# Edge attributes turned by VectorE in 32x32 squares, from rows loaded to two sets of partitions

## Chip, core and metric

The kernel runs on one core of one Trainium2 chip. The metric is the device time of one execution in microseconds; the lower the better. The median of three runs of the kernel before is 1333.0 us (1331.73 to 1334.65).

Names used below: PE or TensorE multiplies matrices, and its weight loads (PEld) run beside the matmuls; DVE or VectorE works on elements; ACT or ScalarE computes activations and copies; POOL or GpSimd here issues the gathers; SP or SyncE issues most of the other transfers. PSUM is the memory that TensorE writes[...].

## What is computed

A graph layer over 8192 nodes of 256 features and 131072 edges of 64 attributes. The edges are sorted by their target node.

```python
ea  = edge_attr @ w_e + b_e                       # 131072 x 256
msg = relu(x[src] + ea)                           # rows of x gathered by source node
agg = segment_sum(msg, dst, num_segments=8192)    # summed by target node
t = x + agg
h_local = bn1(relu(t @ w1 + b1) @ w2 + b2 + x)
# attention within graphs of 32 nodes, 4 heads
q, k, v = split(x.reshape(256, 32, 256) @ in_w.T + in_b)
h_attn = bn2((softmax(q k' / 8) v) @ out_w.T + out_b + x)
out = h_local + h_attn
out = bn3(out + relu(out @ m_w1 + m_b1) @ m_w2 + m_b2)
return layernorm(x + out)
```

All arrays are float32.

## The kernel before

**Two kinds of work.** The edges are cut into 128 blocks of 1024 (NB, BE), the nodes into 16 chunks of 512 (NCH, CH). A block is 4 groups (NH) of 256 edges; a group is 128 partitions by TJ = 2 edges. The node work of a chunk is attention (attention_front, attention_back) and, after all sums for its nodes have been placed, the dense layers (dense).

**An edge block, in five steps.** gather (L129) issues 8 indirect loads on POOL, each of 128 rows of x, into one of 4 buffers xs. load_edges (L144) issues on SP, for every second block, one load of 512 KB that brings the attributes of two blocks, 512 contiguous bytes (two edges) for each partition and group; there are two such buffers. edge_transpose (L163) turns the four 128x128 squares of a block by TensorE into one PSUM bank (tag "sm"), from where ScalarE copies them to eaT, of which there are two buffers. edge_products (L451) multiplies eaT, half of the partitions for each of the two edges, with w_e (matmuls at L459) into two-bank tiles "pe", of which there are two; for the first NX = 20 blocks it also adds b_e by matmuls at L467, and later blocks gather from xb, a copy of x with b_e added that copy_load and copy_store make in the first 14 blocks. edge_messages (L472) adds the gathered rows to the products on VectorE (L481, two additions of 128x1024 per block, four of 128x512 in the last) and applies relu on ScalarE (L485). edge_sums (L497) adds the messages of equal targets by matmuls with a 0/1 matrix oh (edge_hot, L490), into a bank of the same tag "sm"; ScalarE copies them to ws. edge_place (L516) spreads these sums over node columns by matmuls at L522 into a bank l2 of its own, and VectorE adds them to xT, the turned x of the chunk (L532).

**Order.** TensorE's order is written out by hand for the whole loop, that of VectorE and ScalarE up to block NV = 26; elsewhere a scheduler orders the instructions when the kernel is built. The loop goes in rounds of two blocks up to block 119 and of one block from 120 on (NS = 8). A round consists of products, messages, the sums of the blocks of the round before, products and messages of the second block, node work, transposes for two blocks ahead, placing of the sums, and node work.

**The planner.** Node work is cut into steps that are Python generators; each step yields its TensorE time in the planner's own microseconds (1.7 for a layer's 512 columns, for instance). `work.run(us)` takes steps from four streams in turn until the time asked for is used up. A step that yields REST lets its stream rest for two calls of run. Each round asks for 0.3 of its share, then twice 0.1 around the transposes and the placing, then 0.5 (PER = 5.1 for a block). A chunk's dense layers are ready when the last block that touches its nodes has been placed.

**PSUM.** Two banks "at" for node work, two tiles "pe" of two banks, one bank "sm" shared by edge_transpose and edge_sums, one bank l2.

**Start.** The source nodes of the first two blocks are loaded to the layout of the gathers by two small DMAs (L61). Those of all other blocks are loaded as rows, converted (srcf), turned by TensorE and copied to srci; the targets likewise (dstf to rel).

Of the kernel before, what the change touches and what calls it, by code (L numbers as in the profile page):

```python
# [18 lines left out]
P = 128  # L19
# [8 lines left out]
TB = NH * TJ  # L28
NPB = N // NB
# [22 lines left out]
def gnn_kernel(ctx: ExitStack, tc: tile.TileContext, x, src, dst, edge_attr, w, out):  # L52
# [7 lines left out]
    for b in range(ND):  # L60
        (nc.sync, nc.scalar)[b].dma_start(  # L61
            srcd[:, b * NH : (b + 1) * NH, :], src[b * BE : (b + 1) * BE].rearrange("(g p j) -> p g j", p=P, j=TJ)
        )
# [56 lines left out]
    def bank():  # L120
        return pps.tile([P, CH], FP, name="at", tag="at", bufs=2)
# [22 lines left out]
    def load_edges(b):  # L144

        if b % 2:
            return
        ea = epool.tile([P, 2, NH, TJ * ED], FP, name="ea", tag="ea", bufs=2)
        nc.sync.dma_start(
            ea.rearrange("p s h d -> p (s h) d"),  # L150
            edge_attr[b * BE : (b + 2) * BE, :].rearrange("(g p j) d -> p g (j d)", p=P, j=TJ),
        )
        for s in range(2):
            ea_of[b + s] = ea[:, s]
# [4 lines left out]
    load_edges(2)  # L159
# [3 lines left out]
    def edge_transpose(b):  # L163
        ea = ea_of.pop(b)
        tp = pps.tile([P, NH, P], FP, name="tp", tag="sm", bufs=1)
        for h in range(NH):
            nc.tensor.transpose(tp[:, h, :], ea[:, h, :], ident)  # L167
        eaT = epool.tile([P, NH, P], FP, name="eaT", tag="eaT", bufs=2)
        nc.scalar.copy(eaT, tp)  # L169
        eaT_of[b] = eaT  # L170

    with tc.tile_pool(name="setup", bufs=1) as sp:
# [17 lines left out]
        edge_transpose(0)  # L190
        edge_transpose(1)
        srcf = npool.tile([P, NH, P, TJ], FP, name="srcf", tag="zT")
        nc.vector.tensor_copy(srcf.rearrange("s h p j -> s (h p j)"), srci_r)
        for h in range(NH):
            ps = bank()[:, : TJ * NB].rearrange("p (j s) -> p j s", j=TJ)
            for j in range(TJ):
                nc.tensor.transpose(ps[:, j, :], srcf[:, h, :, j], ident)
# [33 lines left out]
        dstf = npool.tile([P, NH, P, TJ], FP, name="dstf", tag="oT")  # L231
        nc.vector.tensor_copy(dstf.rearrange("s h p j -> s (h p j)"), dsti_r)

        dst3 = dstf.rearrange("s h p j -> s h (p j)")
# [5 lines left out]
        for h in range(NH):  # L240
            ps = bank()[:, : TJ * NB].rearrange("p (j s) -> p j s", j=TJ)
            for j in range(TJ):
                nc.tensor.transpose(ps[:, j, :], dstf[:, h, :, j], ident)
# [207 lines left out]
    def edge_products(b):  # L451

        eaT = eaT_of.pop(b)
        for h in range(0, NH, 2):
            pe = bank2().rearrange("p i (u c) -> p i u c", u=2)
            for u in range(2):
                for i in range(2):
                    rows = slice(i * ED, (i + 1) * ED)
                    nc.tensor.matmul(  # L459
                        pe[:, i, u, :], eaT[rows, h + u, :], we[rows, :],  # L460
# [9 lines left out]
            pe_of[b, h] = pe  # L470

# [343 lines left out]
```

## Time and profile before

One execution was profiled: it took 1332.57 us, and its span from the first instruction to the last is 1330.7 us.

| engine | busy us | share of the span | instructions |
|---|---|---|---|
| PE | 1234.3 | 93% | 8307 |
| PEld | 783.6 | 59% | 8307 |
| DVE | 712.2 | 54% | 1202 |
| ACT | 658.7 | 49% | 959 |
| POOL | 983.9 | 74% | 1032 |

| row of the profile | count | busy us | mean us of one |
|---|---|---|---|
| L134 gather (from xb; from x 160 more) | 864 | 824.9 | 0.955 |
| L481 message addition, DVE | 258 | 304.7 | 1.211 |
| L459 edge product, PE | 2048 | 262.3 | 0.391 (overlapping) |
| L504 sums, PE | 2048 | 124.6 | 0.382 (overlapping) |
| L169 copy of turned attributes, ACT | 128 | 74.3 | 0.581 |

The DMA engines moved 206.8 MB, 155 GB/s over the span.

How to read this: busy time is time in which an instruction of the engine was running; matmuls overlap, so that the mean duration of one times their count is more than their busy time. A timeline line gives start, duration, engine, line, operation, what it writes and reads, and in brackets how long the engine was idle before it and which event ended that. "issue" means that the profile shows no event. Several instructions of one kind can stand in one line (x4); the duration is then that of all. An engine that is idle costs nothing where another sets the pace.

### The profile page before, as it was taken

The numbers are of one execution on the slowest core, as the hardware profiler recorded it, in microseconds if no ns is written. First come the engines' busy times: TensorE is split into PE (matmuls) and PEld (weight loads), VectorE is DVE, ScalarE is ACT, GpSimd is POOL, SyncE is SP. The second block draws the span as 40 slices with busy tenths as digits, with TensorE's granted clock in tenths as the row PEclk, the third lists the DMA queues.
The fourth block names the chain that finished last, engine by engine and source line by source line (L and its number), as shares of the span: only waits on it lengthen the run. The fifth ranks groups of instructions, "written<-read, shape, count | busy, mean of one in ns | idle before, by whom it ended". The sixth has DMA issues, their size and how long they took to land.

```text
span 1330.7 us, 21178 instructions
## 1 busy us (share of the span) xinstructions
PE 1234.3 (93%) x8307; PEld 783.6 (59%) x8307; DVE 712.2 (54%) x1202; ACT 658.7 (49%) x959; POOL 983.9 (74%) x1032
## 2 busy tenths in 40 slices
PE   4998979999999999899899999999898998989997
PEld 3766756655555556556556565555555565655665
DVE  4566554555537464644637464564636446454654
ACT  2535344465546455455546555463545445544443
POOL 7777777777777777777777777777777777777770
PEclk9998989999999999999999999999999999999999
DMA  8788655454545454454545454454445445444540
GB/s 279 251 277 272 198 149 151 135 159 130 168 137 153 135 166 126 132 170 125 165 137 150 138 169 136 121 169 138 151 138 151 135 138 150 136 136 139 159 116 30
DMA packets 140613, 206.77 MB, mean 155 GB/s; under 512 B 19646, under 2 KB 103900, under 8 KB 139740
## 3 DMA queue, kind: packets, MB, share of 16 engines
q0 software_dynamic: 49152, 134.28, 35.0%
q1 hardware_dynamic: 89468, 69.76, 16.8%
q10 hardware_dynamic: 1888, 1.32, 0.3%
q8 instruction: 67, 1.10, 0.3%
q14 instruction: 38, 0.31, 0.1%
HBM read 188.51 MB, written 16.78 MB: 154 GB/s over the span
## 4 chain that ended last, share of the span: by engine, by line
PE 56%; POOL 17%; issue 9%; DVE 8%; ACT 6%; DMA 4%; DVEq 0%; ACTq 0%; POOLq 0%
POOL xs L134 17%; PE at L391 16%; PE pe L459 11%; PE at L294 6%; PE pw L504 5%; PE l L522 3%; PE at L372 3%; DVE msg L481 3%; PE at L308 3%; PE tp L167 3%; PE pe L467 3%; DMA xs<-xb,srci 2%; PE at L360 2%; ACT pr L335 2%; DVE bd L352 1%
## 5 line engine op out<-in xcount | busy, mean ns | idle before, releaser
L134 POOL DMA_INDIRECT xs<-xb,srci x864 | 824.9, 955 | 263.8 <-issue 249.8
L485 ACT ACTIVATE msg<-msg 128x1024 f32<-128x1024 f32 (+1 forms) x258 | 270.9, 1051 | 329.5 <-DVE msg L481 320.7
L481 DVE TENSOR_TENSOR msg<-pe,xs 128x1024 f32<-128x1024 f32 (+1 forms) x258 | 304.7, 1211 | 174.5 <-PE pe L459 72.3
L459 PE MATMUL pe<-we,eaT 64*128 64x256 f32 x2048 | 262.3, 391 | 12.0 <-DVE msg L481 11.1
L459 PEld LDWEIGHTS pe<-we,eaT 64*128 64x128 f32 x2048 | 187.3, 187 | 99.7 <-issue 43.5
L134 POOL DMA_INDIRECT xs<-in_x_dram,srci x144 | 142.1, 987 | 45.3 <-issue 41.1
L391 PE MATMUL at<-hA,mw 128*128 128x512 f32 (+2 forms) x304 | 123.6, 533 | 3.4 <-ACT xT L284 2.0
L504 PE MATMUL pw<-msg,oh 128*32 128x256 f32 x2048 | 124.6, 382 | 0.0
L169 ACT COPY eaT<-tp 128x512 f32<-128x512 f32 x128 | 74.3, 581 | 100.0 <-PE tp L167 99.4
L294 PE MATMUL at<-xT,inT 128*128 128x512 f32 x256 | 122.7, 605 | 1.1 <-ACT xT L284 1.1
L391 PE MATMUL at<-m,mw 128*128 128x512 f32 (+2 forms) x304 | 117.4, 530 | 1.4 <-ACT m L407 1.4
L532 DVE TENSOR_TENSOR xT<-l,xT 128x352 f32<-128x352 f32 (+4 forms) x98 | 43.2, 463 | 96.0 <-PE l L522 96.0
L167 PEld LDWEIGHTS tp<-ident,ea 128*128 128x128 f32 x512 | 63.8, 144 | 49.9 <-issue 39.3
L504 PEld LDWEIGHTS pw<-msg,oh 128*32 128x32 f32 x2048 | 59.6, 109 | 54.6 <-issue 21.9
L167 PE MATMUL tp<-ident,ea 128*128 128x128 f32 x512 | 80.0, 280 | 11.8 <-DMA ea<-in_edge_attr_dram 6.1
L522 PEld LDWEIGHTS l<-oh,ws 128*128 128x128 f32 x512 | 74.1, 191 | 14.9 <-issue 13.5
L522 PE MATMUL l<-oh,ws 128*128 128x160 f32 x512 | 81.8, 301 | 0.5 <-ACT ws L510 0.5
L391 PEld LDWEIGHTS at<-m,mw 128*128 128x128 f32 x304 | 53.8, 190 | 48.0 <-issue 43.8
L391 PEld LDWEIGHTS at<-hA,mw 128*128 128x128 f32 x304 | 52.6, 190 | 49.1 <-issue 39.2
L294 PEld LDWEIGHTS at<-xT,inT 128*128 128x128 f32 x256 | 46.1, 192 | 50.2 <-issue 47.2
L391 PE MATMUL at<-xT,w 128*128 128x512 f32 (+2 forms) x152 | 64.8, 558 | 10.1 <-DVE y L431 4.7
L391 PE MATMUL at<-h,w 128*128 128x512 f32 (+2 forms) x152 | 65.5, 554 | 9.1 <-ACT h L398 6.4
(109 smaller groups left out, 1286.9 us busy)
## 6 DMA issues: line engine op xcount, KB each, us to landing
ea<-in_edge_attr_dram SPq DMA_DIRECT2D x64, 512.0 KB
xs<-xb,srci POOLq DMA_INDIRECT x864
xn<-in_x_dram SPq DMA_DIRECT2D x16, 512.0 KB
out_dram<-y SPq DMA_DIRECT2D x14, 512.0 KB
xp<-in_x_dram SPq DMA_DIRECT2D x10, 512.0 KB
xb<-xp SPq DMA_DIRECT2D x10, 512.0 KB
xp<-in_x_dram SPq DMA_DIRECT2D x3, 1024.0 KB
xb<-xp SPq DMA_DIRECT2D x3, 1024.0 KB
```

The source lines that it names most:

```text
L134: nc.gpsimd.indirect_dma_start(out=xs[:, h, j, :], out_offset=None, in_=x if b < NX else xb[:, :], in_offset=bass.IndirectOffsetOnAxis(ap= ...
L167: nc.tensor.transpose(tp[:, h, :], ea[:, h, :], ident)
L169: nc.scalar.copy(eaT, tp)
L294: nc.tensor.matmul(ps, inT[:, k, o * P : (o + 1) * P], xT[:, k, :], start=(k == 0), stop=(k == KC - 1))
L308: nc.tensor.matmul(ps[:, (t - t0) * C : (t - t0 + 1) * C], xT[:, k, t * P : (t + 1) * P], inT[:, k, 2 * C :], start=(k == 0), stop=(k == K ...
L391: nc.tensor.matmul(ps, wt[:, k, o * P : (o + 1) * P], act[:, k, :], start=(k == 0), stop=(k == nk - 1))
L459: nc.tensor.matmul(pe[:, i, u, :], eaT[rows, h + u, :], we[rows, :], start=(b >= NX or u == 0), stop=(b >= NX), skip_group_check=True,)
L481: nc.vector.tensor_add(msg[:, hs].rearrange("p u i c -> p i u c"), pe[:, :, u : u + n, :], xs[:, hs].rearrange("p u i c -> p i u c"),)
L485: nc.scalar.activation(msg[:, hs], msg[:, hs], AF.Relu)
L504: nc.tensor.matmul(pw[h * WN : (h + 1) * WN, i, :], oh[:, h * TJ + j, :], msg[:, h, j, :], start=(j == 0), stop=(j == TJ - 1), skip_group_ ...
L522: nc.tensor.matmul(l2[:, k, i * NPB : i * NPB + WB], ws[:, i, k * P : (k + 1) * P], oh2[:, i, :], start=(i == 0 and k == 0), stop=(i == la ...
L532: nc.vector.tensor_add(xT, l2[:, :, a - n : z - n], xT)
```

## The change

load_edges now loads one block at a time, in four DMAs of 32 partitions. Each DMA brings all four groups of the edges of one j, 1 KB (four edges) per partition and group. The same rows go to two sets of 32 partitions, once for the first 32 attributes (i = 0) and once for the last 32 (i = 1); the second set lies 32 columns further left, so that one access pattern finds the right half on all partitions. The loaded bytes are twice those of before. edge_transpose is now one VectorE instruction that turns all 32x32 squares of the block from ea to eaT; TensorE and ScalarE have no part in it. With the new layout, partition p of a group of 128 edges stands for edge r*4+m and no longer for pairs of edges, so the source and target indices are loaded and turned in the matching order.

The transposes are issued right behind the products that free their eaT buffer (next_edges), and the load for two blocks later behind them. The bank "sm" is gone: edge_sums and edge_place share the one bank of tag "pw", and "at" has three banks. The two calls `work.run(0.1 * per)` are one call `work.run(0.2 * per)`.

```diff
+QR = 32
+EQ = P // QR
...
     for b in range(ND):
-        (nc.sync, nc.scalar)[b].dma_start(
-            srcd[:, b * NH : (b + 1) * NH, :], src[b * BE : (b + 1) * BE].rearrange("(g p j) -> p g j", p=P, j=TJ)
-        )
+        for m in range(EQ):
+            (nc.sync, nc.scalar)[m % 2].dma_start(
+                srcd[m * QR : (m + 1) * QR, b * NH : (b + 1) * NH, :],
+                src[b * BE : (b + 1) * BE].rearrange("(g j r m) -> m r g j", j=TJ, r=QR, m=EQ)[m],
+            )
...
     def bank():
-        return pps.tile([P, CH], FP, name="at", tag="at", bufs=2)
+        return pps.tile([P, CH], FP, name="at", tag="at", bufs=3)
...
     def load_edges(b):
-        if b % 2:
-            return
-        ea = epool.tile([P, 2, NH, TJ * ED], FP, name="ea", tag="ea", bufs=2)
-        nc.sync.dma_start(
-            ea.rearrange("p s h d -> p (s h) d"),
-            edge_attr[b * BE : (b + 2) * BE, :].rearrange("(g p j) d -> p g (j d)", p=P, j=TJ),
-        )
-        for s in range(2):
-            ea_of[b + s] = ea[:, s]
+        ea = ea_of[b] = epool.tile([P, QR + NH * EQ * ED], FP, name="ea", tag="ea", bufs=2)
+        for j in range(TJ):
+            for i in range(ED // QR):
+                p0, c0 = j * ED + i * QR, (1 - i) * QR
+                nc.sync.dma_start(
+                    ea[p0 : p0 + QR, c0 : c0 + NH * EQ * ED].rearrange("r (g d) -> r g d", g=NH),
+                    edge_attr[b * BE : (b + 1) * BE, :].rearrange("(g j r m) d -> j r g (m d)", j=TJ, r=QR, m=EQ)[j],
+                )
...
     def edge_transpose(b):
         ea = ea_of.pop(b)
-        tp = pps.tile([P, NH, P], FP, name="tp", tag="sm", bufs=1)
-        for h in range(NH):
-            nc.tensor.transpose(tp[:, h, :], ea[:, h, :], ident)
-        eaT = epool.tile([P, NH, P], FP, name="eaT", tag="eaT", bufs=2)
-        nc.scalar.copy(eaT, tp)
-        eaT_of[b] = eaT
+        eaT = eaT_of[b] = epool.tile([P, NH * EQ, QR], FP, name="eaT", tag="eaT", bufs=2)
+        nc.vector.transpose(eaT, ea[:, QR:].rearrange("p (g d) -> p g d", d=ED)[:, :, :QR])
...
-        edge_transpose(0)
-        edge_transpose(1)
-        srcf = npool.tile([P, NH, P, TJ], FP, name="srcf", tag="zT")
-        nc.vector.tensor_copy(srcf.rearrange("s h p j -> s (h p j)"), srci_r)
+        for b in range(2):
+            edge_transpose(b)
+            load_edges(b + 2)
+        srcf = npool.tile([P, NH * TJ, EQ, QR], FP, name="srcf", tag="zT")
+        nc.vector.tensor_copy(srcf, srci_r.rearrange("s (t r m) -> s t m r", r=QR, m=EQ))
...
+    def next_edges(b):
+        if b < NB:
+            edge_transpose(b)
+        if b + 2 < NB:
+            load_edges(b + 2)
...
-        pw = pps.tile([P, 2, C], FP, name="pw", tag="sm", bufs=1)
+        pw = pps.tile([P, 2, C], FP, name="pw", tag="pw", bufs=1)
...
-        l2 = pps.tile([P, KC, C], FP, name="l2", tag="l2", bufs=1)
+        l2 = pps.tile([P, KC, C], FP, name="l2", tag="pw", bufs=1)
...
             for i in blocks:
-                if i % 2 == 0 and i + 4 < NB:
-                    load_edges(i + 4)
                 if i + 2 < NB:
                     gather(i + 2)
...
             edge_products(b)
+            next_edges(b + 2)
             edge_messages(b)
             if waiting:
                 sums = edge_sums(waiting)
             waiting = list(blocks)
             if n == 2:
                 edge_products(b + 1)
+                next_edges(b + 3)
                 edge_messages(b + 1)
...
-            for k, i in enumerate(blocks):
-                if i + 2 < NB:
-                    edge_transpose(i + 2)
-                    if k == 0:
-                        work.run(0.1 * per)
-                if sums and k == 0:
-                    edge_place(*sums)
-                    placed, sums = sums[0][-1], None
-                    work.run(0.1 * per)
+            if sums:
+                edge_place(*sums)
+                placed, sums = sums[0][-1], None
+            work.run(0.2 * per)
             for i in blocks:
                 edge_hot(i)
             work.run(0.5 * per)
```

The targets (dstf) are converted and turned like the sources; edge_products reads the same 128 columns per group from the new eaT.

More of the change, by code (lines that the diff above doesn't have):

```diff
@@ L158, in gnn_kernel @@
     gather(1)
-    load_edges(2)
+    load_edges(1)
     eaT_of = {}
@@ L196, in gnn_kernel @@
             for j in range(TJ):
-                nc.tensor.transpose(ps[:, j, :], srcf[:, h, :, j], ident)
+                nc.tensor.transpose(ps[:, j, :], srcf[:, h * TJ + j].rearrange("s m r -> s (m r)"), ident)
             nc.vector.tensor_copy(srci[:, :, h * TJ : (h + 1) * TJ].rearrange("p s j -> p j s"), ps)
@@ L228, in gnn_kernel @@
         turned(out_r, outT, KC)
-        dstf = npool.tile([P, NH, P, TJ], FP, name="dstf", tag="oT")
-        nc.vector.tensor_copy(dstf.rearrange("s h p j -> s (h p j)"), dsti_r)
-        dst3 = dstf.rearrange("s h p j -> s h (p j)")
+        dstf = npool.tile([P, NH * TJ, EQ, QR], FP, name="dstf", tag="oT")
+        nc.vector.tensor_copy(dstf, dsti_r.rearrange("s (t r m) -> s t m r", r=QR, m=EQ))
+        dst3 = dstf.rearrange("s (h j) m r -> s h (j m r)", j=TJ)
         lo = sp.tile([P, NH], FP, name="lo")
@@ L242, in gnn_kernel @@
             for j in range(TJ):
-                nc.tensor.transpose(ps[:, j, :], dstf[:, h, :, j], ident)
+                nc.tensor.transpose(ps[:, j, :], dstf[:, h * TJ + j].rearrange("s m r -> s (m r)"), ident)
             nc.vector.tensor_copy(rel[:, :, h * TJ : (h + 1) * TJ].rearrange("p s j -> p j s"), ps)
@@ L451, in edge_products @@
     def edge_products(b):
-        eaT = eaT_of.pop(b)
+        eaT = eaT_of.pop(b).rearrange("p (h m) r -> p h (m r)", h=NH)
         for h in range(0, NH, 2):
@@ L459, in edge_products @@
                     nc.tensor.matmul(
-                        pe[:, i, u, :], eaT[rows, h + u, :], we[rows, :],
+                        pe[:, i, u, :], eaT[rows, h + u], we[rows, :],
                         start=(b >= NX or u == 0), stop=(b >= NX), skip_group_check=True,
```

## Prediction

> **What bounds the kernel now.** I read the page's first part, then who waited for whom on GpSimd (POOL), then POOL's timeline from its first gather to its last, then VectorE beside it, and last the timeline of the end.
>
> ```profile
> PE 1234.3 (93%) x8307; PEld 783.6 (59%) x8307; DVE 712.2 (54%) x1202; ACT 658.7 (49%) x959; POOL 983.9 (74%) x1032
> ...
> L134 POOL DMA_INDIRECT xs<-xb,srci x864 | 824.9, 955 | 263.8 <-issue 249.8
> ```
>
> TensorE looks like the bound (93%), POOL has 74%. But POOL's busy time leaves out 0.3 us in front of every gather, and those gaps end with no releaser ("issue"). The waits of POOL say the same:
>
> ```profile
> POOL xs L134 <- issue: 295.5, 970, 0.3
> POOL xs L134 <- DVE oh L513: 3.8, 6, 1.7
> ```
>
> 970 of 1024 gathers start 0.3 us behind the one before; all other waits of POOL together are some 17 us, and most of these too are the same 0.3 us under another name. Only one is long: 1.7 us, in front of block 18. In POOL's timeline (start, duration) the first gathers and the last are
>
> ```profile
> 3.31 1.10 POOL L134 DMA_INDIRECT xs<-in_x_dram,srcd  x1 [1.70 <-DMA srcd<-in_src_dram]
> 4.71 0.95 POOL L134 DMA_INDIRECT xs<-in_x_dram,srcd  x1 [0.31 <-issue]
> ```
> ```profile
> 1298.82 0.94 POOL L134 DMA_INDIRECT xs<-xb,srci  x1 [0.30 <-issue]
> ```
>
> One gather each 1.25 us. From 3.31 to 1299.76 are 1296.5 us; 1024 x 1.25 = 1280; the other 16.5 are gathers that took longer and two waits for a free xs buffer. So the time is 3.3 (start) + 1296.5 (gathers) + 30.9 (end) = 1330.7 us, and what the change takes from TensorE counts only where it shortens one of the three. Which gathers take longer? Those that start inside a VectorE operation with two SBUF inputs; four stream transposes in a row hold none:
>
> ```profile
> 61.87 3.42 DVE L552 TENSOR_TENSOR xp<-xp,be 128x2048 f32<-128x2048 f32 x2
> 62.71 2.26 POOL L134 DMA_INDIRECT xs<-in_x_dram,srci  x1 [0.30 <-issue]
> ```
> ```profile
> 173.16 2.85 DVE L352 STREAM_TRANSPOSE bd<-pr 32x512 f32<-32x512 f32 x4
> ```
> ```profile
> 173.07 0.94 POOL L134 DMA_INDIRECT xs<-in_x_dram,srci  x1 [0.30 <-issue]
> 174.31 0.94 POOL L134 DMA_INDIRECT xs<-in_x_dram,srci  x1 [0.30 <-issue]
> ```
>
> The gather at 62.71 ends 0.8 us after the 128x2048 addition does. Start by start along both timelines, the excess over 0.945 us adds up to about 15 us, nearly all such holds; of 36 gathers that start within a transpose of L352, 35 aren't held. The wait at block 18 is VectorE's message for block 14, which ends at 190.76, in a buffer that the gather needs:
>
> ```profile
> 189.54 1.22 DVE L481 TENSOR_TENSOR msg<-pe,xs 128x1024 f32<-128x1024 f32 x1 [0.50 <-PE pe L467]
> ```
> ```profile
> 191.03 0.97 POOL L134 DMA_INDIRECT xs<-in_x_dram,srci  x1 [1.70 <-DVE oh L513]
> ```
>
> The end: a block's last gather ends (935.58 + 0.95 = 936.53, gather 736, block 91), and its second message addition starts when the rows have landed, 1.9 us later.
>
> ```profile
> 935.58 0.95 POOL L134 DMA_INDIRECT xs<-xb,srci  x1 [0.30 <-issue]
> ```
> ```profile
> 938.46 1.23 DVE L481 TENSOR_TENSOR msg<-pe,xs 128x1024 f32<-128x1024 f32 x1 [3.49 <-DMA xs<-xb,srci]
> ```
>
> Before the end, block 127's rows could be used at 1299.8 + 1.9 = 1301.7, but its first message starts at 1303.00 behind TensorE's products:
>
> ```profile
> 1286.23 0.49 DVE L532 TENSOR_TENSOR xT<-l,xT 128x320 f32<-128x320 f32 x1 [1.18 <-PE l L522]
> 1286.78 1.99 PE L391 MATMUL at<-xT,w 128*128 128x256 f32 x8 [0.58 <-DVE xT L532]
> ...
> 1301.82 2.00 PE L459 MATMUL pe<-we,eaT 64*128 64x256 f32 x16
> 1303.00 2.48 DVE L481 TENSOR_TENSOR msg<-pe,xs 128x512 f32<-128x512 f32 x4 [0.52 <-PE pe L459]
> ...
> 1307.43 1.16 PE L391 MATMUL at<-xT,w 128*128 128x128 f32 x8 [0.76 <-DVE xT L532]
> ```
>
> TensorE works from 1286.78 to 1325 nearly without a gap, in a fixed order, set off by the xT addition at 1286.23 that places block 124.
>
> [...] the page's slices show 0.8 to 0.9 busy in the first 120 us and about 0.5 later.
>
> **The change, part by part.**
>
> ```profile
> L167 PE MATMUL tp<-ident,ea 128*128 128x128 f32 x512 | 80.0, 280 | 11.8 <-DMA ea<-in_edge_attr_dram 6.1 <-ACT eaT L169 3.5 <-ACT ws L510 2.3
> L169 ACT COPY eaT<-tp 128x512 f32<-128x512 f32 x128 | 74.3, 581 | 100.0 <-PE tp L167 99.4
> L352 DVE STREAM_TRANSPOSE bd<-pr 32x512 f32<-32x512 f32 x64 | 44.9, 701 | 1.0
> ```
>
> 1. TensorE: 512 transposes go. In the chain of waits four of them stand for 0.44 us, so 128 x 0.44 = 56 us of TensorE time, some 0.9 of the 20.2 us in which POOL brings two blocks. ScalarE loses 128 x 0.58 = 74 us. Both lie beside POOL's gathers, so 0 in the middle; what it buys is that TensorE reaches the end with no backlog (4).
>
> 2. VectorE: 128 stream transposes of 512 elements. Nearest row: L352, 32 partitions, 701 ns. If the four quadrants work at once, 0.70 us each, 90 us in all, VectorE 712 -> 802 us (60%). If one after another, 2.8 us, 358 us, 80%. I take 0.70: other VectorE rows with 512 elements cost 0.68 to 0.69 on 128 partitions. Up to block 26 the order is written out: the transpose of b+2 waits for all products of b (it reuses eaT) and stands before the messages of b, so each message is about 0.7 to 1 us later against its products. Queued behind: the additions that free product banks, then the relus and sums. TensorE meanwhile has 1.9 us of sums, so it loses at most 0.3 us a pair, against 0.9 gained. Holds on POOL by the transposes: 0, from the 35 of 36; up to 0.2 each (25 us) if 128 partitions were different, for which nothing speaks.
>
> 3. Loads: 4 x 128 KB per block in place of half of a 512 KB load, so 512 loads on SP for 64, each some 0.4 to 0.5 us of issue (SP's rows at L149): 230 us of an idle queue. Bytes: 33.5 MB more, 26 GB/s over the middle on 150. They are issued two blocks (20 us) ahead. Cost 0 after block 20, since half the DMA time is free; before it see the slower rival.
>
> The start: the index load for the first two blocks becomes four loads, two on each queue for block 0. The second of a queue issues about 0.45 us later (L61's own issue time), so gather 0 comes at 3.8: +0.5, up to +1.5 if the first gather waits for all eight. The other setup (srci for block 2) has 7 us in hand: its cast at L198 ends at 17.0, gather 16 starts at 23.97. The setup's casts read with a stride and VectorE's two transposes stand among them; at most 2 to 3 us, less than 7. Block 4's buffer is free 6.7 us before it is needed (message of block 0 ends at 37.2, gather at 43.97).
>
> POOL's waits: 1.4 us (1.7 less the usual 0.3) at block 18 and 0.5 at block 22. By then TensorE has saved 14 x 0.44 = 6 us, less 2 to 3 for a later setup and 1 for the transpose: the waits go. -1.9, and 0 if they stay. Sum for the gathers: +0.5 - 1.9 = -1.4; the last gather ends at 1298.4. Holds by two-input operations shift with the phase of the two engines: 0, +-2.
>
> 4. The end. Third bank: TensorE's waits for a node bank's evacuation are small (the largest rows are 11 and 10 us; it is idle for 96 us in all, 17 of them in the first 40 us), and no more than 1 us in the end; I take 0. The sums and placing in one bank: placing needs ws, which is copied out of that bank, and the next sums need messages that stand on VectorE behind the xT additions; cost 0. The planner is called three times per round and not four, so its order moves. Stepping through its yields (order only) gives in both versions nothing to do in round 124 until block 124 is placed; in the changed one, the output step of chunk 15's first half (DVE y and statistics) comes before block 127's products, one half-chunk step (0.85) moves ahead, and 1.7 of the third quarter's work before the last sums, leaving 0.85 less after the last placing.
>
> So with no backlog the set-off point is block 125: its second message at 1279.8 (end of its gathers) - 1.4 + 1.9 = 1280.3, done 1281.5, then the xT addition behind it (0.5), TensorE at 1282.1 for 1286.78: -4.7. From there the chain is the same work to the last placing. The 0.85 less behind it (0.9 us with its gaps) gives -5.6 in all, 1330.7 -> 1325.1. Check against the landing: products of 127 at about 1298, last rows usable at 1300.3, four additions of 0.62 from 1299.7: done 1302.2, before the xT addition's turn; the landing doesn't bind further. Check against TensorE: block 120 to 125 save 6 x 0.44 = 2.6, plus two waits of transposes behind ws (1.46 and 0.81 at 1280 and 1285), which is 4.9: just enough.
>
> **Rivals.** No change: TensorE's backlog (messages 9 us behind the gathers at blocks 120 to 123) isn't worked off, or VectorE's additional 0.7 a block eats what TensorE gains, and the end keeps its 30.9; start +0.5, waits -0.5: 1332.6. For it: POOL can't go faster. Against: TensorE's chain loses 0.44 a block with nothing in its place.
>
> Slower, one mechanism: late edge rows in the first 140 us. DMA share is 0.78 to 0.90 up to 120 us, at 256 to 296 GB/s, with 3 MB of node copies in each pair of blocks on the same SP queue. New loads make 26 GB/s more. If that fills the queues, 14 blocks x 0.26 MB = 3.7 MB at 300 GB/s are 12 us; VectorE, in its written order, waits for the rows in front of the messages, and from the point where they are later than POOL's slack (6.3 us at block 14, 0.3 at block 18) every us moves all later gathers. With all 12 on POOL and 4.2 won at the end: about 1340.5. Against: 20 us of lead and a share below 1.
>
> More than forecast: the last rows, not TensorE, end up as the only limit, or the holds fall by chance; about 1321.
>
> **How the numbers follow.** The profiled execution took 1332.57, 1.9 around its span; 1332.57 - 5.6 = 1327.0. The median of the runs, 1333.0, is 0.4 above it: 1327.4. Chances: forecast 0.60 (own range 1323 to 1330.2), no change 0.20, slower 0.15, more 0.05. A measurement of this kernel tells 0.2% (2.7 us) from no change. Range 1321 to 1334: the slower case is outside. Faster 0.65, same 0.20, slower 0.15.
>
> **What would show it.** First gather at about 3.8; no POOL wait over 0.3; transposes of ea at 0.70 us with no gather stretched in them; last gather's end near 1298; w1 of chunk 15 (L391 behind the xT addition of 124) near 1282; end 26.7 us behind the last gather. It is wrong if POOL shows waits for VectorE messages before block 26, if transposes take 2.8 us, or if the gathers take longer beside denser loads.

## The result: 3.5 us slower

Eleven runs of each kernel: median 1335.8 us with the change (1332.16 to 1339.24), 1332.2 us before (1330.45 to 1335.54). The ratio on record is 1.0033, 95% interval 1.0023 to 1.0042, or 4.4 us; the two medians alone are 3.5 us apart. The forecast was 1327.4 us, range 1321 to 1334.

The profiled execution of the changed kernel took 1339.24 us, the longest of its eleven, so its span of 1337.5 us holds some 3.5 us that the median does not. In the page's first part the change did what it says (the engines' busy time, first line) and cost VectorE what was forecast (the group, second line):

```profile
PE 1193.8 (89%) x7795; PEld 743.4 (56%) x7795; DVE 780.2 (58%) x1330; ACT 587.7 (44%) x831; POOL 986.1 (74%) x1032
...
L169 DVE STREAM_TRANSPOSE eaT<-ea 128x512 f32<-128x512 f32 x128 | 89.9, 702 | 76.4 <-PE pe L459 60.7
```

TensorE lost 40 us of work and is behind less: VectorE's message additions now wait most for gathered rows (97.6 us in sum), before for products (72.3). The 128 transposes cost 702 ns each. POOL still issues one gather per 1.25 us. What changed for the worse stands in its waits, and in its timeline (start, duration):

```profile
POOL xs L138 <- DVE msg L487: 7.1, 13, 3.4
POOL xs L138 <- DMA xs<-xb,srci: 6.1, 20, 0.3
POOL xs L138 <- DVE oh L519: 2.3, 3, 1.6
```
```profile
4.23 1.10 POOL L138 DMA_INDIRECT xs<-in_x_dram,srcd  x1 [2.63 <-issue]
...
48.52 0.95 POOL L138 DMA_INDIRECT xs<-in_x_dram,srci  x1 [3.43 <-DVE msg L487]
...
196.42 0.97 POOL L138 DMA_INDIRECT xs<-in_x_dram,srci  x1 [1.65 <-DVE oh L519]
```

The first gather starts 0.9 us later than before. At 48.52, the first gather of block 4 has waited 3.4 us for the messages of block 0, whose buffer it fills; before, that buffer had been free for 6.7 us. The 1.6 us wait at block 18 (196.42), which the forecast struck out, is still there. VectorE's timeline shows how late the start is; first the changed kernel, then the one before (srcf are the source nodes as float32, srci_r the rows that they are converted from):

```profile
15.66 0.71 DVE L169 STREAM_TRANSPOSE eaT<-ea 128x512 f32<-128x512 f32 x1 [11.19 <-DMA ea<-in_edge_attr_dram]
20.15 0.71 DVE L169 STREAM_TRANSPOSE eaT<-ea 128x512 f32<-128x512 f32 x1 [3.78 <-DMA ea<-in_edge_attr_dram]
22.04 1.07 DVE L193 CAST srcf<-srci_r 128x1024 f32<-128x1024 int32 x1 [1.18 <-DMA srci_r<-in_src_dram]
...
45.93 2.31 DVE L487 TENSOR_TENSOR msg<-pe,xs 128x1024 f32<-128x1024 f32 x2
```
```profile
12.61 0.69 DVE L193 CAST srcf<-srci_r 128x1024 f32<-128x1024 int32 x1 [9.06 <-DMA srci_r<-in_src_dram]
...
34.29 1.23 DVE L481 TENSOR_TENSOR msg<-pe,xs 128x1024 f32<-128x1024 f32 x1 [4.64 <-PE pe L467]
```

The cast of srcf stood at 12.61 before, the first message at 34.29: 9.4 and 11.6 us earlier. What moved it shows in SP's own timeline, here of the changed kernel and then of the one before (time spent includes waits between the loads of a group):

```profile
2.68 10.69 SPq L154 DMA_DIRECT2D ea<-in_edge_attr_dram  x8
13.41 0.44 SPq L176 DMA_DIRECT2D srci_r<-in_src_dram  x1
...
25.91 3.64 SPq L154 DMA_DIRECT2D ea<-in_edge_attr_dram  x8
29.60 0.98 SPq L276 DMA_DIRECT2D xn<-in_x_dram  x2
```
```profile
1.25 1.12 SPq L149 DMA_DIRECT2D ea<-in_edge_attr_dram  x2
3.21 0.61 SPq L177 DMA_DIRECT2D srci_r<-in_src_dram  x1
...
20.29 0.95 SPq L276 DMA_DIRECT2D xn<-in_x_dram  x2
```

Eight loads of edge rows take 10.7 us to issue where two took 1.1, and srci_r stands behind them: 13.41 for 3.21. Eight more stand ahead of the node rows xn: 29.60 for 20.29; of these 9.3 us they take 3.6, and the rest comes from what stands further ahead. The issue of one of the first eight is 0.31 to 0.45 us in six cases, 0.75 and 1.13 in two; the rest are waits on SP. The longest waits of its first 50 us are

```profile
SPq L154 <- DVE eaT L169: 6.9, 1, 6.9
SPq L154 <- DMA in_r<-in_L_gnn_in_w_dram: 3.7, 1, 3.7
SPq L187 <- DMA out_r<-in_L_gnn_out_w_dram: 3.1, 1, 3.1
```

The first of these comes after the setup (46.04, a load for block 4), the third behind srci_r; only the second stands in front of it. What such a wait is for shows in the two traces: the loads of SP's and ScalarE's queue together use eight semaphores, which tell of landings, in turn, and no load of the start is issued before the last load with its semaphore (in the changed kernel the one seven to nine issues before it) has landed, whatever that one loads. Those that had to wait start 0.02 us behind that landing: 12 loads of the changed kernel up to 24.38 us, 7 of the one before up to 18.53. The eighth edge load (13.06) so waits for in_r, 768 KB of attention weights that ScalarE's queue has issued, which has landed at 13.04. What stands behind it on SP waits with it: the semaphore of srci_r had been free since 6.55, and srci_r is issued at 13.41, right behind the eighth edge load.

### The profile page after: what moved, and what is told of

It reads as the page before. It is cut to its first block, busy times and chain, and to the rows that moved or that the text cites. A ratio compares the mean times of both kernels' runs of the same rounds, so it can differ in the third digit from the quotient of the medians.

```text
span 1337.5 us, 21071 instructions
## 1 busy us (share of the span) xinstructions
PE 1193.8 (89%) x7795; PEld 743.4 (56%) x7795; DVE 780.2 (58%) x1330; ACT 587.7 (44%) x831; POOL 986.1 (74%) x1032
## 3 DMA queue, kind: packets, MB, share of 16 engines
q1 hardware_dynamic: 97196, 103.34, 28.9%
## 4 chain that ended last, share of the span: by engine, by line
PE 42%; POOL 23%; issue 12%; DVE 11%; DMA 10%; ACT 2%; DVEq 0%; ACTq 0%; SPq 0%; POOLq 0%
POOL xs L138 23%; PE at L391 14%; PE pe L459 7%; DMA xs<-xb,srci 6%; PE at L294 4%; PE pw L510 4%; DVE msg L487 3%; PE l L528 3%; PE at L372 3%; PE at L308 2%; PE at L360 2%; DMA xs<-in_x_dram,srci 1%; DVE bd L352 1%; PE pe L467 1%; DMA xp<-in_x_dram 1%
## 5 line engine op out<-in xcount | busy, mean ns | idle before, releaser
L487 DVE TENSOR_TENSOR msg<-pe,xs 128x1024 f32<-128x1024 f32 (+1 forms) x258 | 306.5, 1197 | 173.3 <-DMA xs<-xb,srci 97.6
L459 PE MATMUL pe<-we,eaT 64*128 64x256 f32 x2048 | 269.2, 396 | 29.0 <-DVE msg L487 24.6
L459 PEld LDWEIGHTS pe<-we,eaT 64*128 64x128 f32 x2048 | 191.3, 189 | 116.9 <-issue 75.6
L138 POOL DMA_INDIRECT xs<-in_x_dram,srci x144 | 143.3, 995 | 48.4 <-issue 40.5
L169 DVE STREAM_TRANSPOSE eaT<-ea 128x512 f32<-128x512 f32 x128 | 89.9, 702 | 76.4 <-PE pe L459 60.7
L528 PEld LDWEIGHTS l<-oh,ws 128*128 128x128 f32 x512 | 77.0, 194 | 28.9 <-issue 18.2
L391 PE MATMUL at<-xT,w 128*128 128x512 f32 (+2 forms) x152 | 72.9, 623 | 18.6 <-DVE xT L538 18.6
L416 DVE SCALAR_TENSOR_TENSOR zT<-at,s,zT 128x512 f32<-128x512 f32 (+2 forms) x38 | 25.3, 665 | 87.4 <-PE at L391 86.8
L297 ACT ACTIVATE qk<-at,vec 128x512 f32<-128x512 f32 x64 | 43.6, 683 | 61.5 <-PE at L294 61.1
```

The costliest lines, as they stand in the source:

```text
L138: nc.gpsimd.indirect_dma_start(out=xs[:, h, j, :], out_offset=None, in_=x if b < NX else xb[:, :], in_offset=bass.IndirectOffsetOnAxis(ap= ...
L169: nc.vector.transpose(eaT, ea[:, QR:].rearrange("p (g d) -> p g d", d=ED)[:, :, :QR])
L297: nc.scalar.activation(qk[:, o, :], ps, AF.Identity, bias=v_("in_b", o))
L391: nc.tensor.matmul(ps, wt[:, k, o * P : (o + 1) * P], act[:, k, :], start=(k == 0), stop=(k == nk - 1))
L459: nc.tensor.matmul(pe[:, i, u, :], eaT[rows, h + u], we[rows, :], start=(b >= NX or u == 0), stop=(b >= NX), skip_group_check=True,)
L487: nc.vector.tensor_add(msg[:, hs].rearrange("p u i c -> p i u c"), pe[:, :, u : u + n, :], xs[:, hs].rearrange("p u i c -> p i u c"),)
```

## The theories and the runs

Three theories for the loss. A: the late start. SP's small loads make the setup 9 to 12 us later, and POOL waits at blocks 4 and 18: 3.4 + 1.6 us, less the usual 0.3 each, are 4.4 us. B: the end. TensorE, now idle for 11% of the span where it was for 7% before, is granted a lower clock (0.962 in the mean for 0.986), and its last work takes longer. C: the doubled bytes slow the gathers all along.

The runs fell on different chips. On one, the kernel before itself takes 2016 to 2100 us, because TensorE stands still between matmuls that wait for nothing shown, as here between transposes of the setup that otherwise follow each other at once (TensorE's timeline, the changed kernel):

```profile
26.06 2.05 PE L207 MATMUL at<-ident,in_r 128*128 128x128 f32 x8 [0.72 <-issue]
30.27 0.69 PE L207 MATMUL at<-ident,in_r 128*128 128x128 f32 x2 [2.17 <-issue]
35.86 0.69 PE L207 MATMUL at<-ident,in_r 128*128 128x128 f32 x2 [4.90 <-issue]
```

VectorE's, ScalarE's and POOL's instructions last what they last elsewhere (in e1, from 600 to 640 us: a transpose of ea 0.70 us, a message addition 1.18 to 1.21, a relu 1.06, a gather 0.94 to 0.95; in the changed kernel above 0.70, 1.21, 1.06 and 0.95). In the changed kernel there, TensorE is busy for 226 us more and idle between instructions for 437 us more than above, which are the 663 us that its span is longer; POOL waits 562.8 us in sum for messages, for 7.1 above. There TensorE decides and not POOL; ratios of that chip are a question of their own and are told last. First the runs on chips where the kernel before takes 1332 us.

### Reduced kernels: the start

Four kernels with less work on TensorE, which leave out a part of the result (here of the dense layers; input, value and output projections likewise; of the sums only j = 0):

```diff
-            for k in range(nk):
-                nc.tensor.matmul(
-                    ps, wt[:, k, o * P : (o + 1) * P], act[:, k, :], start=(k == 0), stop=(k == nk - 1)
-                )
+            nc.tensor.matmul(ps, wt[:, 0, o * P : (o + 1) * P], act[:, 0, :], start=True, stop=True)
```

> The kernel before with TensorE's work cut, since on this chip TensorE stands still between matmuls and decides: the linear layers (in, out, w1, w2, m_w1, m_w2 and the values) use only the first 128 of their input rows, and the sums only half of a block's messages; that part of the result is left out. Gathers, edge rows, products, messages, buffers, loads and all orders are as before; 1880 of 8307 matmuls go. It is the base for the next three. All theories: POOL decides again, about 1.25 us per gather, 1310 to 1345 us, no wait of POOL over 2 us behind block 26. If it is above 1400, TensorE still decides and the four runs say nothing on POOL.

> The changed kernel with the same part of TensorE's work left out as in l0_before_lite. Theory A (late start): POOL's waits at block 4 and about block 18 are there, last gather 3 to 5 us later than in l0, time 3 to 5 us above l0. Theory B (the loss of the changed kernel is made in its end, by TensorE's half clock): with so little work TensorE waits for gathers in both, so the end costs alike and the time is within 1.5 us of l0. Theory C (the doubled bytes slow the gathers): 3 to 5 us above l0, spread over the span and not at blocks 2 to 18.

> The changed kernel with the new order of the start (srci_r and dsti_r loaded ahead of the edge rows, srcf cast ahead of the first two transposes) and the same part of TensorE's work left out as in l0_before_lite. Theory A: POOL's waits at blocks 4 and 18 go, time within 1.5 us of l0 and 2.5 to 5 us below l1. Theory C: within 1 us of l1, above l0. Theory B: l0, l1 and l2 within 1.5 us of each other.

> The kernel before with its first two loads of edge rows cut into four each, and the same part of TensorE's work left out as in l0_before_lite. Theory A: cast of srcf near 22 us for 12.6, POOL waits for srci at block 2 (1.6 us as in the full kernel) and for messages at block 4 (0.5 to 3 us), last gather 1.5 to 4.5 us later than in l0, and the time as much above it. Theories B and C: within 1 us of l0.

The start order of l2 (the setup's own lines go; VectorE's cast of srcf moves ahead of its first two transposes as well):

```diff
+    srci_r = npool.tile([P, BE], I32, name="srci_r", tag="y")
+    dsti_r = npool.tile([P, BE], I32, name="dsti_r", tag="h1")
+    nc.sync.dma_start(srci_r, src.rearrange("(s e) -> s e", s=NB))
+    nc.sync.dma_start(dsti_r, dst.rearrange("(s e) -> s e", s=NB))
     gather(0)
     load_edges(0)
     gather(1)
     load_edges(1)
```

The small first loads of l3:

```diff
-        nc.sync.dma_start(
-            ea.rearrange("p s h d -> p (s h) d"),
-            edge_attr[b * BE : (b + 2) * BE, :].rearrange("(g p j) d -> p g (j d)", p=P, j=TJ),
-        )
+        n = 4 if b < 4 else 1
+        for q in range(n):
+            r = slice(q * P // n, (q + 1) * P // n)
+            nc.sync.dma_start(
+                ea.rearrange("p s h d -> p (s h) d")[r],
+                edge_attr[b * BE : (b + 2) * BE, :].rearrange("(g p j) d -> p g (j d)", p=P, j=TJ)[r],
+            )
```

| kernel | median us | ratio to before, interval | srcf cast | first message | POOL's wait in the start | last gather ends |
|---|---|---|---|---|---|---|
| l0 before | 1324.4 | 0.9939 (0.9925 to 0.9953) | 12.2 | 33.9 | none | 1296.0 |
| l1 changed | 1327.2 | 0.9965 (0.9953 to 0.9978) | 21.8 | 46.0 | 2.7, block 4 | 1302.0 |
| l2 changed, srci_r first | 1325.0 | 0.9948 (0.9933 to 0.9964) | 6.8 | 45.1 | 1.5, block 4 | 1299.8 |
| l3 before, small first loads | 1322.7 | 0.9929 (0.9912 to 0.9946) | 23.0 | 42.4 | 1.6, block 2 | 1297.2 |

l1 is 2.8 us above l0, a little under what A and C expected. l2 gives back 2.2 of it, just clear of the spread of these runs (some 1.9), so the order of two loads and one cast is worth most of the loss here. In the profiles half of that is POOL's shorter wait at block 4 (1.54 us for 2.68), the other half fewer lengthened gathers, which may be chance. That speaks against C; against B it does so for these kernels only, in which TensorE has less to do in the end. l2's first message did not come forward, as A had expected: TensorE's products of block 0 stand in its order behind the turns of xn, and xn's loads stood on SP at 28.9 behind vec_r and the loads of blocks 2 and 3. l3 shows that cutting the loads alone, with the same bytes, moves the cast by 10.8 us and the first message by 8.4 (of 12.1 in l1). A's price for it was wrong, and late loads alone did not bring the loss about: the messages of block 0 still came in time for block 4, POOL lost only 1.3 us at block 2, waiting for srci, and the time isn't above l0. Eight us late still fit ahead of block 4, POOL itself being 1.3 us later; twelve do not.

### The whole start put in order

SP's order is now srci_r, dsti_r, rows of block 0, vec_r, rows of block 1, xn, and only then the rows of blocks 2 and 3:

```diff
     gather(0)
     load_edges(0)
     gather(1)
+    vec_r = npool.tile([nrows, P], FP, name="vec_r", tag="pr")
+    for v in VECS:
+        r, n = col[v]
+        nc.sync.dma_start(vec_r[r : r + n, :], w[v].rearrange("(r p) -> r p", p=P))
     load_edges(1)
...
             if c < 2:
                 next(front)
+                if c == 1:
+                    load_edges(2)
+                    load_edges(3)
                 next(front)
```

> The changed kernel, start order alone: on SP first srci_r and dsti_r, then the edge rows of block 0, the twelve short vec_r loads, the rows of block 1, the node rows xn of the first two chunks, and only then the rows of blocks 2 and 3 (which wait for VectorE's first transposes); the srcf cast stands ahead of those transposes. In l2_start_order_lite srcf was cast at 6.8 but the first message still came at 45.1, because xn stood on SP behind vec_r and eight loads of blocks 2 and 3 (issued at 28.9). Theory A (late start): xn issued near 15 to 20, first message at 31 to 37 (45.9), no POOL wait above 0.5 at block 4 and 18; the time falls 2.5 to 5 us against the changed kernel's 1.0033, to a ratio of 0.9995 to 1.0015. Theory B (end): 1.0025 or above.

The cast of srcf stands ahead of the first two transposes, as in l2. Measured: 1331.7 us in 22 runs, ratio 1.0001 (0.9994 to 1.0009). SP issues xn at 23.94 and no longer at 29.60, and the first message comes at 41.24, later than A expected but 4.7 us earlier than in the changed kernel. That is enough; VectorE's first message, and POOL's waits by name:

```profile
41.24 2.32 DVE L486 TENSOR_TENSOR msg<-pe,xs 128x1024 f32<-128x1024 f32 x2
```
```profile
POOL xs L138 <- DMA xs<-in_x_dram,srci: 3.1, 8, 0.9
POOL xs L138 <- DVE msg L486: 2.4, 8, 0.3
```

No gather waits over 0.3 us for a message; one in block 12 waits 0.9. From 1.0033 to 1.0001 are 0.0032 of 1332, or 4.3 us (by the two intervals 2.7 to 5.9; by the medians 3.6); the two waits taken away had been 4.4. So the order of the start accounts for the loss. One reservation: the changed kernel as it is was not run on e6's chip, so each is measured against the kernel before on its own chip. It is also shown that hardly anything of the forecast gain is left once the start is repaired: the change then costs between -0.8 and +1.2 us.

### The end and the clock

Four transposes per block are put back on TensorE, in the product bank, where the products overwrite them; e7 does so on top of the new start, from block 112 on (its edit is shown; e3b has no condition).

```diff
             for u in range(2):
+                if b >= 112:
+                    nc.tensor.transpose(pe[:, 0, u, :P], eaT[:, h + u], ident)
+            for u in range(2):
                 for i in range(2):
```

> The changed kernel with four 128x128 transposes per block put back on TensorE (into the product bank, overwritten by the products; the output is unchanged), on a chip that runs the kernel before in 1332 us. Theory B (TensorE with gaps is clocked down and pays in the end): granted clock from 0.963 to 0.98 or above, no half-speed window in the last 50 us, ratio 1.0005 to 1.002. Theory A: 1.0025 to 1.0045, the granted clock as it may be. A third outcome, above 1.005, would say that TensorE's relief was worth something.

> e6_start_order_full with the four transposes per block put back on TensorE from block 112 on alone (into the product bank, overwritten; the output is unchanged), so that TensorE has fewer gaps in the last 160 us. Theory B: fewer half-speed windows behind 1280 us, and 1 to 3 us less than e6. Theory A: e6's time within 0.7 us, or above it by what TensorE does longer (up to 1 us).

Ratios 1.0399 (1.0381 to 1.0417) and 1.0095 (1.0076 to 1.0114): the third outcome, and not a test of B; e7 missed what both theories expected. The work put back is more than was meant. TensorE's timeline of one block, in e3b and then in the kernel before:

```profile
905.99 0.44 PE L457 MATMUL pe<-ident,eaT 128*128 128x128 f32 x2
906.36 1.13 PE L461 MATMUL pe<-we,eaT 64*128 64x256 f32 x8
907.42 0.44 PE L457 MATMUL pe<-ident,eaT 128*128 128x128 f32 x2
907.79 1.14 PE L461 MATMUL pe<-we,eaT 64*128 64x256 f32 x8
```
```profile
904.84 0.60 PE L167 MATMUL tp<-ident,ea 128*128 128x128 f32 x4
...
910.52 2.00 PE L459 MATMUL pe<-we,eaT 64*128 64x256 f32 x16
```

From 905.99 to the next instruction (908.86) are 2.87 us, where 16 products alone take 1.93 (910.52 to 912.45): 0.94 us a block, 120 us in all. The four transposes before took 0.44 in one row (904.84 to 905.28). TensorE's gaps in the changed kernel add up to 114 us. It becomes the bound: the last gather ends at 1328.3, and the end takes 52 us more. In e7, 16 blocks of 0.94 us are 15 us; the end is 38.5 us for e6's 28.9. So of work put on TensorE in the last 160 us two thirds come back in the end: TensorE has little slack there, in the changed kernel too.

What the clock costs is seen only in the profiled executions. In the changed kernel two half-speed windows of 3.41 us fall into the end; eight matmuls set off by the placing of block 124 take 3.46 us to the next instruction, where e6 takes 1.83 (first line, and second):

```profile
1289.65 3.62 PE L391 MATMUL at<-xT,w 128*128 128x256 f32 x8 [1.95 <-DVE xT L538]
1293.11 2.29 PE L391 MATMUL at<-h,w 128*128 128x256 f32 x8
```
```profile
1283.47 1.99 PE L390 MATMUL at<-xT,w 128*128 128x256 f32 x8 [0.83 <-DVE xT L537]
1285.30 2.29 PE L390 MATMUL at<-h,w 128*128 128x256 f32 x8
```

In the two traces the granted clock changes between full and half in windows of 3.41 us and multiples of it (the last of a profile is cut short by its end): 19 stretches at half speed with 104 us in the changed kernel, 10 with 40 us before. In the 3.41 us ahead of each of the 29, TensorE was busy for 0 to 52% of the time (over the spans for 89 and 93%); three windows with 44 to 51% were followed by full speed. In e3b, with the transposes back on TensorE, the mean granted clock is 0.979, in e6 0.964. The changed kernel's end is 31.8 us and e6's, without such a window before its last matmul, 28.9; their orders are the same. Whether the median run of the changed kernel has such windows in its end isn't known: what B costs in the end is left open, at most the 2.9 us between these two. As a cause of the whole loss B falls with e6: its clock is as low as the changed kernel's (0.959 to 0.967 in its 22 runs, 0.962 to 0.967 in the other's 11; before, 0.983 to 0.988 on e6's chip), and yet it is some 4 us faster.

### The bytes

The kernel before with the changed kernel's loads from block 4 on; half of the bytes go to a tile that nothing reads (the load of the rows that are used is cut into four as well):

```diff
+        if b >= 4:
+            spare = epool.tile([P, NH * 4 * ED], FP, name="spare", tag="spare", bufs=1)
+            for s in range(2):
+                for j in range(TJ):
+                    p0 = (2 * j + s) * 32
+                    nc.sync.dma_start(
+                        spare[p0 : p0 + 32, :].rearrange("r (g d) -> r g d", g=NH),
...
```

> The kernel before with the changed kernel's DMA work from block 4 on (128 KB loads, four per block, 512 KB per block, half of it into a tile that nothing reads), on a chip that runs the kernel before in 1332 us. Theory C (bytes or SP's issues slow the gathers or their rows): ratio 1.0015 or above. Theories A and B: within 0.0008 of 1.

Ratio 1.0031 (1.0012 to 1.0050), as C had it, but for a reason that is the experiment's own. One wait of POOL makes it in the profiled execution, at the first gather that reads xb (POOL's timeline; then SP's, of this kernel and of the one before):

```profile
217.90 0.94 POOL L134 DMA_INDIRECT xs<-xb,srci  x1 [6.72 <-DMA ea<-in_edge_attr_dram]
```
```profile
194.43 18.04 SPq L161 DMA_DIRECT2D spare<-in_edge_attr_dram  x10
212.51 1.68 SPq L566 DMA_DIRECT2D xb<-xp  x1
```
```profile
198.87 0.32 SPq L553 DMA_DIRECT2D xb<-xp  x1
```

The last store of xb is issued at 212.51, for 198.87, since it stands on SP behind ten spare loads that wait for one another's tile. (The profile names the landing that came last, a load of ea; that the gather needs this store follows from the program.) The last gather ends 6.4 us later than before, which is this wait less the usual 0.3; beside it nothing is slower: the excess of gathers over 0.945 us is 15.6 us in sum, 15.2 before, with a DMA share of 0.76 (0.49 before, 0.67 in the changed kernel) from 300 to 400 us. In the changed kernel that store is issued at 202.83, in time. So the bytes as such do not slow the gathers; a place in SP's queue did, once more.

### The chip on which TensorE stands still

The first seven runs and the last three fell on it. The edits of e1 and e2 are those of l2 and l3 in the full kernels, e3 and e4 those of e3b and e4b.

> The changed kernel with the order of the start alone altered: the loads of srci_r and dsti_r are issued on SP ahead of the eight loads of edge rows, and the cast of srcf stands ahead of VectorE's first two transposes. Theory A (the loss comes from the late start: 8 small loads ahead of srci_r make the setup 11 us later, so that POOL waits 3.4 us at block 4 and 1.6 us at block 18): cast of srcf near 12 us (22.0), first message near 35 to 38 (45.9), no POOL wait over 0.5 us at block 4 and 18, last gather 3 to 4.5 us earlier than 1305.7, median 1331 to 1333 where the changed kernel has 1335.8. Theory B (the loss comes from the end, where TensorE now idles and runs at half clock): setup earlier, but the median stays at 1335 or above, with the same half-speed windows in the end. Theory C (the doubled bytes of the edge rows slow the gathers all along): the median stays above 1334, gathers' gaps and holds as in the changed kernel.

> The kernel before with its first two loads of edge rows (512 KB each) cut into four of 128 KB each, same bytes: the first 1 MB comes in 8 loads as in the changed kernel, nothing else altered. Theory A: srci_r is issued behind them 8 to 10 us later than before (13 us for 3.2), the first message moves from 34.3 to 42 or later, POOL waits 2 to 4 us at block 4; median 1334.5 to 1336.5 for 1332.2. Theories B and C: no change, within 1 us of 1332.2.

> The changed kernel as it is, so that the other runs have it beside them. On a chip that runs the kernel before in about 1332 us: ratio 1.0023 to 1.0042 as at first, with the cast of srcf at 22 us and POOL's waits of 3.4 and 1.6 us at blocks 4 and 18. On a chip that runs it in about 2088, where TensorE stands still between matmuls and decides: TensorE's removed work counts at full, so 0.968 to 0.98 as with the new start order (0.970, 0.973), and the start order itself is worth no more than its own 10 us: 0.97 to 0.978.

> e6_start_order_full with the index rows of the first two blocks in one tile each, so that the first gather waits for the four loads of block 0 and not for all eight. If the first gather waits for the whole tile: it starts at 3.5 to 3.9 us where e6 has 4.3, the last gather comes as much earlier, and the time falls by 0.4 to 0.8 us (below what is told apart with certainty); if it waits for block 0's own loads already: 4.2 to 4.4 and no change.

> e6_start_order_full with the PSUM banks of the kernel before: two node banks, and sums and placing in a bank each. The forecast put both bank edits at 0: within 0.8 us of e6. If the third bank matters (TensorE's waits for evacuations of node banks come back): more than 1 us above e6, most of it in the end; if sums and placing in one bank cost (the 0.8 to 1.5 us in which TensorE waits for ScalarE's copy of the sums in the end): below e6.

> e6_start_order_full with the planner's call of 0.2 behind the placing divided in two again, 0.1 ahead of it and 0.1 behind it, as in the kernel before. In the changed kernel TensorE now reaches the placing with nothing behind the sums and waits for ScalarE's copy (0.95 to 1.5 us in the end of e6); a step of 0.1 ahead of it can cover this copy. If that wait counts: 0.5 to 2.5 us below e6, the end shorter than e6's 28.9 us. If POOL's gathers set the pace and the order in the end is no better: within 0.7 us of e6.

The last three start from e6:

```diff
-    srcd = const.tile([P, ND * NH, TJ], I32, name="srcd")
+    srcd = [const.tile([P, NH, TJ], I32, name=f"srcd{b}") for b in range(ND)]
```
```diff
-        return pps.tile([P, CH], FP, name="at", tag="at", bufs=3)
+        return pps.tile([P, CH], FP, name="at", tag="at", bufs=2)
...
-        l2 = pps.tile([P, KC, C], FP, name="l2", tag="pw", bufs=1)
+        l2 = pps.tile([P, KC, C], FP, name="l2", tag="l2", bufs=1)
```
```diff
+            work.run(0.1 * per)
             if sums:
                 edge_place(*sums)
                 placed, sums = sums[0][-1], None
-            work.run(0.2 * per)
+            work.run(0.1 * per)
```

| kernel | ratio to before there, interval | before there, us |
|---|---|---|
| e1, and again | 0.9698 (0.965 to 0.9746), 0.9729 (0.9682 to 0.9776) | 2087.7 |
| e2, and again | 1.0027 (1.0008 to 1.0047), 1.0014 (0.9979 to 1.0049) | 2087.7 |
| e3 | 0.9911 (0.988 to 0.9941) | 2087.7 |
| e4 | 1.0034 (1.0008 to 1.006) | 2087.7 |
| e5, the changed kernel | 0.9891 (0.985 to 0.9931) | 2016.2 |
| e8 | 0.9644 (0.9601 to 0.9687) | 2099.8 |
| e10 | 0.9729 (0.9684 to 0.9775) | 2099.8 |
| e11 | 0.9638 (0.9594 to 0.9682) | 2099.8 |

On this chip the change is a gain: with TensorE as the bound, its removed work counts. Before itself moves there by 4% from one set to another, so e1 and e5 are not to be set against each other; e5 gains less than was expected of it (0.968 to 0.98). Within the last set, to which e6 itself doesn't belong, the banks as before (a bank is a tile of 512 float32 per partition here) are 23 us above e8 and 20 above e11 (2048.7 against 2025.6 and 2028.6; six runs each, the intervals of the ratios touch), and the divided call of the planner makes no difference to e8. What both are worth where POOL sets the pace is left open. What precedes TensorE's trouble can be read as elsewhere: e1 casts srcf at 7.8, e2 at 22.7, as l2 and l3 do; and e8's first gather starts at 4.38 us, so it does not wait for the second block's indices, and the 0.9 us lost at the start is block 0's own four loads.

## Why the forecast was wrong, by its steps

**The step that failed** is the start: "The setup's casts read with a stride and VectorE's two transposes stand among them; at most 2 to 3 us, less than 7." Measured: 9.4 us at the cast, 11.6 at the first message, for the 7 us in hand. The casts and transposes themselves cost as said (1.07 for 0.69, 0.71 twice). What was missing is the queue: the part on loads priced 512 of them as "230 us of an idle queue" and looked only at blocks loaded two ahead, where that holds. In the start SP isn't idle, and the eight loads stand in front of srci_r and eight more in front of xn. l2 and e6, which alter this order and the place of one cast, give back 2.2 us of the reduced kernel's 2.8 and 4.3 of the full one's 4.4.

It isn't the whole miss. A gain of 5.6 us was forecast, and with the start repaired none is to be seen (1.0001). By e6's profile, 1.0 of it went by the end of the last gather (1299.4 for 1298.4) and 2.2 in the end, as shown below; the rest isn't located.

**POOL's waits**, -1.9, came out at +2.5: 3.4 and 1.6 at blocks 4 and 18, less 0.3 each, for 1.4 and 0.5 at blocks 18 and 22 before. With the start repaired the waits for messages are gone, so the mechanism was right and its condition was not met.

**The first gather**: +0.5 forecast, +0.9 measured, inside the bounds given.

**TensorE**: 56 us were to go, 40.5 of busy time went; the products' group, for one, grew from 262.3 to 269.2.

**VectorE**: 0.70 us per transpose, no hold on POOL. Right: 702 ns, and of 68 gathers that start within one none is longer by more than 0.01 us. In all VectorE is busy for 780 us where 802 were forecast.

**Doubled loads**, 0 behind block 20: right for the changed kernel, as the bytes run shows beside its one wait.

**The end**, -4.2 (26.7 us for 30.9), came out at +0.8 in the changed kernel's profile (two half-speed windows in it) and at -2.0 in e6's; l1 and l2 too have an end that is 1.9 and 1.8 us shorter than l0's. Of the 2.2 us between forecast and e6, 1.8 lie where my sum put nothing. The last gather and the placing of the last sums, in e6 and then before:

```profile
1298.48 0.94 POOL L138 DMA_INDIRECT xs<-xb,srci  x1 [0.30 <-issue]
...
1312.95 0.71 PE L527 MATMUL l<-oh,ws 128*128 128x160 f32 x4
```
```profile
1298.82 0.94 POOL L134 DMA_INDIRECT xs<-xb,srci  x1 [0.30 <-issue]
...
1314.46 0.71 PE L522 MATMUL l<-oh,ws 128*128 128x160 f32 x4
```

The set-off point was nearly right: 16.3 us ahead of the last gather's end by forecast, 15.95 in e6. But I let the work from there to the last placing stay the same and took 0.85 off behind it, though the steps that leave its back move in front of it. In e6, from 1283.47 to the last placing at 1312.95 are 29.5 us (before, 27.7), with a new wait of 0.54 for the output step's work on VectorE among them and a wait of 1.06 for ScalarE's copy of the sums that had been 0.46 (whether from the bank that sums and placing now share isn't shown; the forecast put that at 0); 15.4 follow (16.2).

**The sum**. e6's profile: +1.0 at the start, -1.4 for the gathers, -2.0 for the end, -2.4; yet its median equals that of before within 0.1%. e6's profiled execution is 1.6 us under its median and that of before 0.3 above, which makes up 1.9 of the 2.4; where in the span the other executions differ isn't known, and the shorter end may be less in them. The changed kernel's profile has such an excess as well: 970 of its gathers are longer by some 3 ns each, 2.8 us in sum, where before has 0.35, l1 0.42 and e6 0.55.

**The slower rival** had the right place (before block 26) and the right lever (POOL's slack, from which each us counts), but the wrong mechanism: not full DMA engines, but order on one queue.

No version of the full kernel beats the kernel before where that takes 1332 us; e6 equals it.

## What to carry to other kernels

A load that is split or added is priced not by its bytes alone but by what stands behind it on its queue at that place: in the first 30 us eight small loads in place of two took 10 us more, in the middle they cost nothing. Where another engine sets the pace, as POOL here, removed work was worth at most what it shortened at the two ends, and a step moved from behind the last link to in front of it is not removed. An experiment that adds work needs the same care: the place of the added loads in the queue, and of the added transposes between paired matmuls, made three of these runs (e3b, e4b, e7) measure something else.

## What the hardware showed unasked

- In the start, loads of SP and ScalarE together, which use eight semaphores in turn, were held until the last load with the same semaphore had landed (12 of them in the changed kernel start 0.02 us behind such a landing); a 768 KB load so held SP for 3.7 us, though it was another queue's.
- Four transposes of 128 rows cost 0.44 us where they stand in one row (before), and 0.94 where they stand by twos between products of 64 rows (e3b): 0.37 for each two, and 1.06 instead of 0.97 for each eight products.
- One chip ran the kernel before in 2016 to 2100 us for 1332. In the changed kernel there (e5), TensorE was slower: gaps of up to 5 us between transposes in its setup, and a granted clock of 0.83 (0.96 in the changed kernel's own profile); VectorE's cast of srcf took 1.09 us for 1.07, its transpose of ea 0.71 in both.
